# Four cross-attention layers: masked steps taken four at a time, row maxima and denominators spread by way of DRAM

## The chip, the cores and the metric

The kernel runs on one core of a Trainium2 chip. The metric is the device time of one launch in microseconds (us). The engines are PE (TensorE, the matrix products; its weight loads are a row of their own, PEld), DVE (VectorE), ACT (ScalarE), POOL (GpSimd) and SP (SyncE, which here only issues transfers). PE writes to PSUM alone; POOL cannot reach PSUM.

## The reference

`x` (2048 queries of 256 values) passes through four cross-attention layers with a residual each. The keys and values come from one context of 1601 rows of 512 values. Layers 0, 2 and 3 are alike, each with its own weights, 16 heads of 64:

```python
q = hidden_states @ Wq            # 2048 x 1024
k = encoder_hidden_states @ Wk    # 1601 x 1024
v = encoder_hidden_states @ Wv
logits = jnp.einsum('bhqd,bhkd->bhqk', q, k) * scale
col_bias = col_bias.at[:, token_indices_A].set((-SUPPRESS * suppress_A_in)[:, None])
col_bias = col_bias.at[:, token_indices_B].set((-SUPPRESS * suppress_B_in)[:, None])
probs = jax.nn.softmax(logits + col_bias[None, None, :, :], axis=-1)
out = jnp.einsum('bhqk,bhkd->bhqd', probs, v)
out = out.transpose(0, 2, 1, 3).reshape(B, HW, HEADS * HEAD_DIM) @ Wo + bo + residual
```

Four context columns per layer get a bias that depends on the query's mask. Layer 1 has no mask: it takes an RMS norm of `x`, 16 heads of 16 for the queries and 4 heads for keys and values, and the same softmax and residual. All of it is in float32.

## The kernel before

The masked layers (class `Masked`) are cut into blocks of two heads (`n`, 8 of them) and each block into four units of 512 queries. The 12 special context columns of all layers are appended to the context, so a unit has 1613 keys: 13 chunks of 128 (the last has 77). One chunk of one unit is a step, and step numbers run on from unit to unit over the whole kernel. For each step, in time:

- `front` (L400): PE forms the scores of 128 keys by 2 heads by 512 queries in one PSUM tile `s` (two tiles in all). `front_act` (L421, L417 for the first chunk) has ACT copy them to a tile `p` of a ring of 22 in SBUF; `front_dve` (L429) has DVE keep a running maximum `top` over the chunks, per key row.
- after the last chunk, `top_pe` (L438) transposes `top` in two groups of four, `top_dve` (L443) reduces each to the negative maximum of each query, and `spread_pe` (L449) transposes a broadcast of it with eight products into a PSUM tile `mb`, in which every row holds the maxima of all queries.
- 16 steps after the front, `subtract` (L460, L458 for the first chunk): DVE adds `mb` to `p`. `exc` masks the columns that the layer replaces.
- 18 steps after it, `exp_act` (L466): ACT takes the exponential in place; then `exp_pool` (L474, L472): POOL adds the tile to `sums`.
- 20 steps after it, `attend` (L482): PE multiplies by the values into one PSUM tile `po`. After the last chunk `take` (L489) copies it to `o`.

Denominators follow a unit's end: `den_pe` (L300, through `halves`) forms the column sums of `sums` as 16 narrow products, `den_dve` (L503) takes reciprocals, `den_act` (L507) and `scale_pe` (L515) spread them by four transposes, `scale_dve` (L518) multiplies `o`. `out_pe` (L300) and `out_dve` (L527, L532) project and add to the residual `xT`.

Keys and values of the next block are formed during this one: `fill` cuts that into 14 pieces (`keys`, `values`, L300), which read the transposed context `ctxT`, held whole in SBUF. The queries of the next unit are such a piece too, from a copy of the layer's input in DRAM (`snap`, loaded to `xq` at L892).

The order of every engine's instructions is written out by hand: calls in `pin` keep the program's order. The main loop takes two steps at a time (a pair). In a pair stand: the two fronts; their copies and maxima; one piece (`mid`); the two value products; one more piece (`end`); the exponentials and then the subtractions of older steps. `place` puts a piece at a step or in the first later pair that is free; a pair has one `mid` and one `end`.

The grouped layer (class `Grouped`) has the same loop, but finds the maxima in a first pass of transposed scores (L726, L741) and forms the scores again (L775, L780) for the exponential (L788).

PSUM has room for eight banks: two score tiles and `mb` of two banks each, `po` and a tile `pm` of one, which all pieces share.

Of the kernel before, what the change touches and what calls it, by code (L numbers as in the profile page):

```python
# [26 lines left out]
RING = 22  # L27


SUB, EXP, VAL = 16, 18, 20  # L30
DEN, SCALE, OUT, REST = 34, 36, 38, 43
# [7 lines left out]
def tile_cross_attention_stack(ctx: ExitStack, tc: tile.TileContext, t: dict, out: bass.AP):  # L39
# [26 lines left out]
    ps_s = ctx.enter_context(tc.tile_pool(name="ps_s", bufs=2, space=PSUM))  # L66
    ps_b = ctx.enter_context(tc.tile_pool(name="ps_b", bufs=1, space=PSUM))
# [5 lines left out]

    def wide_tile():
        return ps_b.tile([P, 2, QB], FP, name="mb")
# [16 lines left out]
    ctxT = const.tile([P, NCT, TE], FP, name="ctxT")  # L92
# [134 lines left out]
    def load_context(c):  # L227
        n = min(P, T - c * P)
        rows = ring_tile().rearrange("p a b -> p (a b)")[:, :CT]
        nc.sync.dma_start(out=rows[:n, :], in_=cond[0, c * P : c * P + n, :])  # L230
        pt = ps_m.tile([P, NCT, P], FP, name="pm")
        for k in range(NCT):
            nc.tensor.transpose(pt[:, k, :n], rows[:n, ts(k, P)], ident[:n, :n])
        if c % 2:
            nc.vector.tensor_copy(ctxT[:, :, c * P : c * P + n], pt[:, :, :n])
        else:
            nc.scalar.copy(ctxT[:, :, c * P : c * P + n], pt[:, :, :n])

    def load_extra():
# [5 lines left out]
        nc.vector.tensor_copy(ctxT[:, :, T:TE], pt[:, :, :NX])  # L245
# [29 lines left out]
    max_cols = [const.tile([P, QT, P], FP, name=f"max_cols{i}") for i in range(2)]  # L275

    def grouped_constants():
# [10 lines left out]
        for c in max_cols:  # L288
            nc.gpsimd.memset(c, 0.0)
# [3 lines left out]


# [7 lines left out]
    class Masked:  # L302
# [25 lines left out]
        def fill(self, u):  # L328

            found = []  # L330
            for a, n in spans(TE, 256):
                found.append((NCT * n, *self.keys(u, a, n)))
            for c0 in range(0, NT, 2):
                found.append((NCT * P * min(2, NT - c0), *self.values(u, c0, min(2, NT - c0))))
            return found

        def keys(self, u, a, n):
            box = []

            def pe():  # L340
                pk = ps_m.tile([P, QB], FP, name="pm")
                for k in range(NCT):
                    halves(
                        pk[:, :n], u.wk[:, k, :], ctxT[:, k, a : a + n],
# [9 lines left out]
        def values(self, u, c0, n):  # L354
# [3 lines left out]
            def pe():  # L358
                pv = ps_m.tile([P, 4, P], FP, name="pm")
                for c in range(c0, c0 + n):  # L360
                    for k in range(NCT):
                        halves(
                            pv[:m, c - c0, :],
                            ctxT[:, k, c * P : c * P + m], u.wv[:, k, :],
# [70 lines left out]
        def top_pe(self, w, h):  # L435
            w.pt = ps_m.tile([P, QT, P], FP, name="pm")
            for q in range(QT):
                pin(nc.tensor.transpose(w.pt[:, q, :], w.top[:, h, ts(q, P)], ident))  # L438

        def top_dve(self, w, h):  # L440
            if h == 0:
                w.ntop = small.tile([P, 2, QT], FP, name="ntop")
            pin(nc.vector.tensor_reduce(w.ntop[:, h, :], w.pt, AX.X, ALU.max, negate=True))  # L443

        def spread_pe(self, w):
            w.mb = wide_tile()
            for h in range(2):
                for q in range(QT):
                    pin(nc.tensor.transpose(  # L449
                        w.mb[:, h, ts(q, P)],  # L450
                        w.ntop[:, h, q : q + 1].to_broadcast((P, P)), ident,
                    ))
# [15 lines left out]
        def exp_pool(self, w, c):  # L468
            m = P if c < NT - 1 else TAILX
            if c == 1:  # L470
                w.sums = work.tile([P, 2, QB], FP, name="sums", bufs=1)
# [15 lines left out]
        def take(self, w):  # L487
            w.o = work.tile([P, QB], FP, name="o")
            pin(nc.scalar.copy(w.o, w.po))  # L489

# [43 lines left out]
    class Grouped:  # L534
# [3 lines left out]
        def __init__(self, l):  # L538
            self.l = l
            self.xn = {}  # L540
# [46 lines left out]
        def fill(self, u):  # L587
            found = []
            if u.n == 0:
                for a, n in spans(T, 256):  # L590
                    found.append((NCT * n, *self.keys(u, a, n)))
                for c0, n in [(0, 4), (4, 4), (8, 4), (12, 1)]:
                    found.append((NCT * 64 * n, *self.values(u, c0, n)))
            return found

        def keys(self, u, a, n):
            box = []

            def pe():
                pk = ps_m.tile([P, QB], FP, name="pm")  # L600
                for k in range(NCT):
                    pin(nc.tensor.matmul(
                        pk[:64, :n], self.wk[:, k, :], ctxT[:, k, a : a + n],
# [26 lines left out]
        def values(self, u, c0, n):  # L630
# [3 lines left out]
            def pe():  # L634
# [5 lines left out]
                for c in range(c0, c0 + n):  # L640
                    for k in range(NCT):
                        pin(nc.tensor.matmul(
                            pv[:m, c - c0, :], ctxT[:, k, c * P : c * P + m], self.wv[:, k, :],
# [70 lines left out]
        def front(self, w, i):  # L714
            u = w.u
            s = w.tile()
# [32 lines left out]
        def top_cols(self, w):  # L749
            ntop = small.tile([P, 2, QT], FP, name="ntop")  # L750
            pin(nc.vector.tensor_reduce(ntop, w.top, AX.X, ALU.max, negate=True))
            w.cols = max_cols[w.w % 2]
# [16 lines left out]
        def again(self, w, c):  # L769
            u = w.u  # L770
            m = P if c < NT - 1 else TAIL
            s = w.tile()
# [29 lines left out]
        def take(self, w):  # L802
            if w.pair == 0:
                self.o = work.tile([P, QB], FP, name="o")
# [44 lines left out]
    class Unit:  # L849
        def __init__(self, w):  # L850
# [11 lines left out]

        turn = 0

        def tile(self):
            both = self.alone
            if not both:
                return score_tile() if not self.wide else wide_tile()
            Unit.turn += 1
            return wide_tile() if Unit.turn % 3 == 0 else score_tile()  # L870
# [34 lines left out]
    for c in range(NT):  # L905
        load_context(c)
    load_extra()
# [5 lines left out]
    fill = deque(layers[0].fill(made[0]))  # L913
    for _ in range(len(spans(TE, 256))):
        _, pe, then = fill.popleft()
        pe()
        then()


    class Piece:  # L920
        def __init__(self, cost, pe, act=None, dve=None, pool=None):
            self.cost, self.pe, self.act, self.dve, self.pool = cost, pe, act, dve, pool

    mid, end = {}, {}
    snap_after = {}
    early = {}

    tops = {(NT * w + NT - 1) // 2 + 1 for w in range(NU)}
# [225 lines left out]
```

## Time and profile before

| | us |
|---|---|
| runs | 4931.58, 4923.04, 4931.13 (median 4931.13) |
| profiled execution | 4932.33 |
| its span | 4930.6 |
| layer 0, masked (about) | 90 to 1400 |
| layer 1, grouped (about) | 1400 to 2345 |
| layers 2 and 3, masked (about) | 2300 to 4914 |

How to read the lines shown further on: a row of the timeline has its start in us, its length, engine, line of the kernel, operation, tiles written and read, how many such instructions follow each other and, in brackets, how long the engine was idle before and what ended it. A matrix product in float32 stands there as two instructions. The page's 40 slices give the busy tenths of each engine; `PEclk` is the clock that TensorE was granted:

```
PE   6999999999878989888999999999999999999997
DVE  3788888888876666654788888888888888888896
ACT  2666666667645555555666666667676676666675
POOL 0677677667751221120667776767667676767777
PEclk7999999999989999999999999999999999999998
```

### The profile page before, as it was taken

The numbers are of one execution on the slowest core, as the hardware profiler recorded it, in microseconds if no ns is written. First come the engines' busy times: TensorE is split into PE (matmuls) and PEld (weight loads), VectorE is DVE, ScalarE is ACT, GpSimd is POOL, SyncE is SP. The second block draws the span as 40 slices with busy tenths as digits, with TensorE's granted clock in tenths as the row PEclk, the third lists the DMA queues.
The fourth block names the chain that finished last, engine by engine and source line by source line (L and its number), as shares of the span: only waits on it lengthen the run. The fifth ranks groups of instructions, "written<-read, shape, count | busy, mean of one in ns | idle before, by whom it ended". The sixth has DMA issues, their size and how long they took to land.

```text
span 4930.6 us, 72879 instructions
## 1 busy us (share of the span) xinstructions
PE 4570.5 (93%) x29467; PEld 1955.8 (40%) x29467; DVE 3820.4 (77%) x3771; ACT 3191.3 (65%) x3709; POOL 2912.7 (59%) x1481
## 2 busy tenths in 40 slices
PE   6999999999878989888999999999999999999997
PEld 3443444344333333334443444344434443344432
DVE  3788888888876666654788888888888888888896
ACT  2666666667645555555666666667676676666675
POOL 0677677667751221120667776767667676767777
PEclk7999999999989999999999999999999999999998
DMA  2000000000011000000000000000000000000000
GB/s 81 13 18 19 17 20 18 19 17 23 17 26 36 12 18 17 11 21 20 14 20 17 19 20 18 19 17 20 18 23 13 24 18 20 16 20 20 15 9 18
DMA packets 77334, 98.89 MB, mean 20 GB/s; under 512 B 15481, under 2 KB 54905, under 8 KB 76998
## 3 DMA queue, kind: packets, MB, share of 16 engines
q1 hardware_dynamic: 65766, 80.43, 5.4%
q0 software_dynamic: 9120, 11.72, 1.2%
q8 instruction: 232, 3.80, 0.3%
q10 hardware_dynamic: 2112, 2.10, 0.1%
q14 instruction: 104, 0.85, 0.1%
HBM read 80.80 MB, written 13.40 MB: 19 GB/s over the span
## 4 chain that ended last, share of the span: by engine, by line
PE 66%; DVE 18%; ACT 8%; issue 3%; POOL 3%; DMA 0%; POOLq 0%; SPq 0%; DVEq 0%; ACTq 0%
PE pm L300 20%; PE s L400 16%; PE po L482 14%; DVE top L429 7%; DVE p L460 7%; PE po L796 4%; ACT p L788 3%; POOL sums L472 2%; ACT p L421 2%; PE pm L438 2%; PE s L726 1%; PE s L775 1%; ACT p L466 1%; PE mb L449 1%; PE mb L775 1%
## 5 line engine op out<-in xcount | busy, mean ns | idle before, releaser
L474 POOL TENSOR_TENSOR sums<-sums,p 128x1024 f32<-128x1024 f32 (+1 forms) x1056 | 2502.9, 2370 | 510.5 <-ACT p L466 458.1
L429 DVE SCALAR_TENSOR_TENSOR top<-s,exc,top 128x1024 f32<-128x1024 f32 (+1 forms) x1056 | 1351.7, 1280 | 524.7 <-ACT p L421 498.7
L421 ACT COPY p<-s 128x1024 f32<-128x1024 f32 (+1 forms) x1152 | 1129.8, 1014 | 689.3 <-PE s L400 338.6
L460 DVE SCALAR_TENSOR_TENSOR p<-p,exc,mb 128x1024 f32<-128x1024 f32 (+1 forms) x1152 | 1417.8, 1272 | 0.0
L400 PE MATMUL s<-qT,kT 64*128 64x512 f32 (+1 forms) x4992 | 1282.8, 622 | 92.6 <-DVE top L429 87.6
L466 ACT ACTIVATE p<-p 128x1024 f32<-128x1024 f32 (+1 forms) x1248 | 1253.6, 1057 | 21.8 <-DVE p L460 20.7
L482 PE MATMUL po<-p,v 128*64 128x512 f32 (+1 forms) x4992 | 1215.0, 607 | 6.0 <-ACT p L466 5.2
L400 PEld LDWEIGHTS s<-qT,kT 64*128 64x128 f32 (+1 forms) x4992 | 414.7, 183 | 737.2 <-issue 458.9
L472 POOL TENSOR_TENSOR sums<-p 128x1024 f32<-128x1024 f32 x96 | 226.8, 2363 | 748.0 <-PE pm L300 628.0
L482 PEld LDWEIGHTS po<-p,v 128*64 128x64 f32 (+1 forms) x4992 | 328.6, 138 | 503.6 <-issue 425.5
L741 DVE TENSOR_REDUCE gtop<-s 128x2 f32<-128x1024 f32 x261 | 316.7, 1220 | 128.9 <-PE s L726 127.6
L708 POOL DMA_DIRECT2D qT<-gqueries x256 | 124.0, 499 | 458.4 <-PE s L780 298.0
L788 ACT ACTIVATE p<-s 128x1024 f32<-128x1024 f32 (+1 forms) x267 | 270.0, 1023 | 141.2 <-PE s L780 137.4
L300 PE MATMUL pm<-wv,ctxT 128*64 128x128 f32 (+1 forms) x4992 | 348.5, 276 | 10.6 <-DVE o L518 6.6
L300 PEld LDWEIGHTS pm<-wv,ctxT 128*64 128x64 f32 (+1 forms) x4992 | 279.2, 135 | 161.5 <-issue 67.7
L300 PE MATMUL pm<-ctxT,wk 128*64 128x256 f32 (+1 forms) x2688 | 297.4, 363 | 8.8 <-DVE o L518 5.2
L796 PE MATMUL po<-p,v 128*32 128x512 f32 (+1 forms) x1664 | 248.4, 629 | 1.9 <-ACT rx L808 1.8
L300 PEld LDWEIGHTS pm<-ctxT,wk 128*64 128x64 f32 x2688 | 168.0, 136 | 194.6 <-issue 60.2
L741 DVE TENSOR_REDUCE gtop<-mb 128x2 f32<-128x1024 f32 x123 | 150.2, 1221 | 76.0 <-PE mb L726 75.3
L300 PE MATMUL pm<-o,wo 128*64 128x512 f32 x768 | 204.6, 611 | 4.0 <-DVE xT L532 2.5
L788 ACT ACTIVATE p<-mb 128x1024 f32<-128x1024 f32 (+1 forms) x149 | 152.5, 1024 | 79.2 <-PE mb L780 77.2
L532 DVE TENSOR_TENSOR xT<-pm,xT 128x512 f32<-128x512 f32 x168 | 115.1, 685 | 84.3 <-PE pm L300 84.2
(160 smaller groups left out, 3361.1 us busy)
## 6 DMA issues: line engine op xcount, KB each, us to landing
xq<-snap SPq DMA_DIRECT2D x84, 512.0 KB
qT<-gqueries POOLq DMA_DIRECT2D x256, 32.0 KB, 2.0
wk<-in_L_xattn_Wk_dram SPq DMA_DIRECT2D x24, 256.0 KB
wv<-in_L_xattn_Wv_dram SPq DMA_DIRECT2D x24, 256.0 KB
snap<-xT SPq DMA_DIRECT2D x12, 512.0 KB
gqueries<-xq SPq DMA_DIRECT2D x16, 256.0 KB
kT<-gkeys POOLq DMA_DIRECT2D x16, 200.2 KB, 3.9
wq<-in_L_xattn_Wq_dram SPq DMA_DIRECT2D x24, 128.0 KB
```

The source lines that it names most:

```text
L300: pin(nc.tensor.matmul(to[a:e], weights_ap[:, a:e], moving, **kw))
L400: pin(nc.tensor.matmul(s[:m, h, :], u.kT[r, c * P : c * P + m], w.q[r, :], start=True, stop=(c < NT - 1),))
L421: pin(nc.scalar.copy(w.p[c][:m], w.s[c][:m]))
L429: pin(nc.vector.scalar_tensor_tensor(w.top[:m], w.s[c][:m], self.exc[:m, c : c + 1], before[:m], ALU.add, ALU.max,))
L460: pin(nc.vector.scalar_tensor_tensor(p, p, self.exc[:m, c : c + 1], w.mb[:m], ALU.add, ALU.add))
L466: pin(nc.scalar.activation(w.p[c][:m], w.p[c][:m], AF.Exp))
L472: pin(nc.gpsimd.tensor_tensor(w.sums, w.p[0], w.p[1], ALU.add))
L474: pin(nc.gpsimd.tensor_tensor(w.sums[:m], w.sums[:m], w.p[c][:m], ALU.add))
L482: pin(nc.tensor.matmul(w.po[r, :], w.u.v[:m, c, r], w.p[c][:m, h, :], start=(c == 0), stop=(c == NT - 1),))
L741: pin(nc.vector.tensor_reduce(w.top[:, :, q, k : k + 1], w.s[i], AX.X, ALU.max))
L788: pin(nc.scalar.activation(w.p[c][:m], w.s[c][:m], AF.Exp))
L796: pin(nc.tensor.matmul(w.po[ts(j, 32), :], self.v[:m, c, w.u.g, :], w.p[c][:m, h, :], start=(c < 2), stop=(c >= NT - 2),))
```

## The change

Six things change; the lines below are those that the prediction speaks of, and "..." stands for what is left out.

Where the steps are masked alone, the loop takes four at a time (`quad`): three fronts, the first copy and maximum, the fourth front, the other copies and maxima; four value products with up to four pieces between them; then for each of four older steps the subtraction, the exponential and POOL's addition, right behind each other, with the pieces' own ACT and DVE work between. Around the grouped layer the loop stays with pairs (`pair_of`). Subtraction and exponential both stand 16 steps behind the front.

The maxima are transposed in one group of eight into a score tile, reduced once, written to DRAM and read back by all 128 rows into `mb`, which is now a tile of SBUF. PSUM's freed banks make a third score tile.

The denominators are formed by two products of 512 columns with a weight of ones, copied, sent through DRAM to 128 rows for the reciprocal, and through DRAM again to all rows; POOL multiplies `o` by them. The last block of each layer keeps the old way.

The transposed context goes to DRAM in seven slices; each piece of `fill` gets its slice back by a transfer that ACT issues, two slices ahead. RING is 23; `sums` and `o` have two buffers. The start forms the first keys while it loads the context.

```diff
-RING = 22
-SUB, EXP, VAL = 16, 18, 20
+RING = 23
+SUB, VAL = 16, 20
...
-    ps_s = ctx.enter_context(tc.tile_pool(name="ps_s", bufs=2, space=PSUM))
-    ps_b = ctx.enter_context(tc.tile_pool(name="ps_b", bufs=1, space=PSUM))
+    ps_s = ctx.enter_context(tc.tile_pool(name="ps_s", bufs=3, space=PSUM))
...
+class Fill:
...
+        def load(self):
+            self.cs = slice_tile()
+            n = slices[self.i][1]
+            pin(nc.scalar.dma_start(out=self.cs[:, :, :n], in_=ctxD[self.i]))
...
-        def spread_pe(self, w):
-            w.mb = wide_tile()
+        def top_pe(self, w):
+            w.pt = score_tile().rearrange("p h (q r) -> p h q r", r=P)
             for h in range(2):
                 for q in range(QT):
...
+                    pin(nc.tensor.transpose(w.pt[:, h, q, :], w.top[:, h, ts(q, P)], ident))
+        def top_dve(self, w):
+            ntop = small.tile([P, 2, QT], FP, name="ntop")
+            pin(nc.vector.tensor_reduce(ntop, w.pt, AX.X, ALU.max, negate=True))
+            to = tops[w.w % 2]
+                nc.sync.dma_start(out=to.rearrange("h q p -> p h q"), in_=ntop)
+            w.mb = work.tile([P, 2, QB], FP, name="mb", bufs=2)
+            nc.sync.dma_start(
+                out=w.mb,
+                in_=to.rearrange("h q p -> (h q p)").rearrange("(o f) -> o f", o=1)
+                .to_broadcast((P, 2 * QB)),
+            )
...
-            w.o = work.tile([P, QB], FP, name="o")
+            w.o = work.tile([P, QB], FP, name="o", bufs=2)
...
+        def row_pe(self, w):
+            w.pd = ps_m.tile([P, QB], FP, name="pm")
+            for h in range(2):
+                pin(nc.tensor.matmul(
+                    w.pd[64 * h : 64 * h + 64, :], ones[:, 0:64], w.sums[:, h, :],
+                    start=True, stop=True,
+                ))
+        def row_act(self, w):
+            pin(nc.scalar.copy(rows, w.pd))
+            nc.sync.dma_start(
+                out=to[0], in_=rows.rearrange("(h r) q -> h r q", r=64)[:, 0, :]
+            )
+            nc.sync.dma_start(out=w.d8, in_=to[0].rearrange("h (p j) -> p h j", j=QT))
+        def row_dve(self, w):
+            pin(nc.vector.reciprocal(w.d8, w.d8))
+            nc.sync.dma_start(out=to[1].rearrange("h (p j) -> p h j", j=QT), in_=w.d8)
+            for h in range(2):
+                nc.sync.dma_start(
+                    out=w.rx[64 * h : 64 * h + 64, :],
+                    in_=to[1][h : h + 1, :].to_broadcast((64, QB)),
+                )
+        def row_pool(self, w):
+            pin(nc.gpsimd.tensor_tensor(w.o, w.o, w.rx, ALU.mult))
...
+    def quad(q):
...
+        for f in fronts[:3]:
+            f[0].layer.front(*f)
+        for f in fronts[:1]:
+            copies(f)
+        for f in fronts[3:]:
+            f[0].layer.front(*f)
+        for f in fronts[1:2]:
+            copies(f)
+        if soon_top:
+            top.layer.top_pe(top)
...
+        def exponent(i):
+            for f in subs[i : i + 1]:
+                f[0].layer.subtract(*f)
+                f[0].layer.exp_act(*f)
+                f[0].layer.exp_pool(*f)
+        order = [(turns[i], i) for i in sorted(after)]
+        for i in range(5):
+            for turn, at in order:
+                if turn == i:
+                    upto(at)
+                    piece = after[at]
+                    if piece.dve:
+                        piece.dve()
+                    if piece.act:
+                        piece.act()
...
+            if i < 4:
+                exponent(i)
+        if top and not soon_top:
+            top.layer.top_pe(top)
+            top.layer.top_dve(top)
```

## The prediction

> **What bounds the kernel now.** I read the page's busy rows first, then two stages of equal work, then one pair of steps in order of time. Columns of the stage rows: stage, its us, busy us (instructions) of PE, weight load, DVE, ACT, POOL, then TensorE's granted clock, DMA share, GB/s.
>
> ```profile
> PE 4570.5 (93%) x29467; PEld 1955.8 (40%) x29467; DVE 3820.4 (77%) x3771; ACT 3191.3 (65%) x3709; POOL 2912.7 (59%) x1481
> 2505.40:2666.10 160.70, 154.09 (x1018) 65.74 (x1016) 134.63 (x124) 111.48 (x131) 112.72 (x49) 1.00 0.07 19
> 1500.00:2130.00 630.00, 564.05 (x3576) 238.51 (x3572) 408.94 (x463) 360.81 (x402) 129.94 (x230) 0.95 0.08 17
> ```
>
> The second row is one head pair of a masked layer: four units of 13 steps, 160.7 us, 40.2 a unit, 12.36 per four steps. PE is busy for 154.1 of it (38.5 a unit), DVE for 134.6. The third is the grouped layer; its loops stay as they are.
>
> ```profile
> 2514.44 1.99 PE L400 MATMUL s<-qT,kT 64*128 64x512 f32 x8
> 2515.50 2.46 DVE L460 SCALAR_TENSOR_TENSOR p<-p,exc,mb 128x1024 f32<-128x1024 f32 x2
> 2515.67 1.93 ACT L421 COPY p<-s 128x1024 f32<-128x1024 f32 x2 [1.85 <-PE s L400]
> 2516.36 1.95 PE L300 MATMUL pm<-ctxT,wk 128*64 128x256 f32 x16
> 2517.88 2.66 DVE L429 SCALAR_TENSOR_TENSOR top<-s,exc,top 128x1024 f32<-128x1024 f32 x2
> 2518.14 1.89 PE L482 MATMUL po<-p,v 128*64 128x512 f32 x8
> 2518.62 2.00 ACT L466 ACTIVATE p<-p 128x1024 f32<-128x1024 f32 x2
> 2519.95 1.09 PE L449 MATMUL mb<-ident,ntop 128*128 128x128 f32 x8
> 2520.97 1.99 PE L400 MATMUL s<-qT,kT 64*128 64x512 f32 x8
> ```
>
> PE follows itself without a hole from 2514.44 to 2520.97: the pair is paced by PE. DVE subtracts while the scores run; the exponentials at 2518.62 belong to earlier subtractions, so no engine waits in a circle.
>
> **What PE saves.** Per unit: the spread L449 (2519.95 to 2520.97, 1.02); the scale transposes L515 (0.66, and a change of shape, about 0.2 since scores take 1.92 to the next group but 4 x 0.43 of streaming); half the score/value changes (one of 0.2 saved per four steps, 0.65); the second group of top transposes (0.2). The denominators' 32 column products took 1.10 and become two 512-wide ones at 0.86. Together 2.9: 38.5 becomes 35.6 a unit.
>
> **What takes PE's place: a circle through ACT and DVE.** Before, an exponential ran two steps after its subtraction. Now ACT's order in four steps is copy x4, exp x4, DVE's is max x4, subtract x4, and exp 3 stands ahead of the next four's copy 0. The built order also says what waits: a max waits for the copy of its tile, an exp for its subtraction. So: copy 0 (1.01, L421), 0.06 of semaphore, three maxima 1.38 apart (two at 2517.88 take 2.66, 1.28 the last), 1.20 from the fourth to the first subtraction, three subtractions 1.19 apart (two at 2515.50 take 2.46) and the last 1.27, then 0.06 and exp 3 at 1.06. 1.07 + 4.14 + 1.20 + 3.57 + 1.27 + 1.12 = 12.37. That is as long as four steps take today, with PE no longer the reason. Over four units (13 quads): 160.8; plus four output additions between subtractions at 0.7 (L532 0.685), four reciprocals at 0.2, two wide reductions ahead of a max at 1.22 (L741's form; the other two fall while DVE waits for copy 0), one 0.6 for an L489 copy ahead of a late copy; less the maxima that each unit's first chunk does not have (0.25 to 1.38 by position, 3.4 in all): 164.0 against 160.7.
>
> **What mb in SBUF costs.** mb moves from PSUM to SBUF, so all 13 subtractions of a unit read two tensors of SBUF while POOL adds. The trace has that form once, L675 (xT and parts, both SBUF); the lines are DVE, then POOL, at two places.
>
> ```profile
> L675 DVE SCALAR_TENSOR_TENSOR xq<-xT,normw,parts x8: 737/752/2822, 1349.2 to 1505.4; 128x512 f32<-128x512 f32 x8
> 1349.23 1.98 DVE L675 SCALAR_TENSOR_TENSOR xq<-xT,normw,parts 128x512 f32<-128x512 f32 x1
> 1348.32 2.34 POOL L474 TENSOR_TENSOR sums<-sums,p 128x1024 f32<-128x1024 f32 x1 [4.88 <-ACT p L466]
> 1350.74 2.67 POOL L474 TENSOR_TENSOR sums<-sums,p 77x1024 f32<-77x1024 f32 x1
> 1462.69 0.75 DVE L675 SCALAR_TENSOR_TENSOR xq<-xT,normw,parts 128x512 f32<-128x512 f32 x1
> L474 POOL TENSOR_TENSOR sums<-sums,p x1056: 2335/2369/2705, 136.9 to 4910.8; 128x1024 f32<-128x1024 f32 x160, 77x1024 f32<-77x1024 f32 x16
> ```
>
> Alone it takes 0.75. At 1349.23 it meets an addition that ends at 1350.66 and itself ends at 1351.21, 0.55 later, just its stream: it had waited. The next addition, at 1350.74, takes 2.67 for 2.37: POOL waited for DVE, and went on 0.38 after its own last end. The second L675 then waited for that addition (2.82). So they take turns, an operation at a time, the waiting one next. L429 and L460 read one SBUF and one PSUM tensor; 1.28 and 1.27, they never show this. A 1024-wide subtraction so ends 1.08 after the addition that it met, and holds POOL for 0.38 + 0.53 = 0.91.
>
> A quad, from its first subtraction: subtractions at 0, 1.19, 2.38; exp 0 ends 2.39, addition 0 asks at 2.45, just after subtraction 2, and runs 3.4 to 5.8; subtraction 3, at 3.57, meets it and ends at 6.88, not 4.84: +2.04. The other three additions (7.1) fit the 7.5 until the next first subtraction. With an output addition between subtractions 1 and 2, addition 0 is first: subtraction 2 ends at 5.90, addition 1 has waited and takes until 8.1, subtraction 3 ends at 9.18, not 5.56: +3.6. Nine quads and four: 18.4 + 14.4. The new multiplication on POOL (1.26, L809's row) comes behind the three and reaches 0.7 into the next subtractions, once a unit: 2.8. Four units: 164.0 + 32.8 + 2.8 = 199.6, which is 38.9 more. Ends: nothing (POOL always yields), and two additions in every quad, 13 x 4.34 and the output additions hidden: 220.4.
>
> The Trainium skill, "SBUF — State Buffer", section "SBUF: two separate sides", speaks against this edit: a VectorE operation with two SBUF inputs and a GpSimd operation that reads SBUF lock each other out, whoever starts first for its whole instruction. With whole instructions a unit would need 13 x 1.27 + 12 x 2.37 + 1.26 = 46.2 of that lock; the 0.91 of the rows makes it 41.5, already over 40.2.
>
> **Edits costed at nothing.** Each with its cover. (a) Maxima by way of DRAM: reduce, 1024 values of 4 bytes out (L471), 512 KB in (L473), both on SP. Nearest rows: columns of 256 values land after 4.9 to 5.7, a 200 KB stack after 3.9, so about 9.6; cover is three steps, 9 or more at the new pace; uncovered it stops DVE at a unit's first subtraction, and the exps behind it: 0 to 3 a unit, taken as 0. (b) Denominators: five more transfers on SP, ahead of xq's and the weights' loads, which are asked 20 steps early; the waits lie in front of POOL's multiplication, two quads later; behind that stand the next additions, and PE's output product (L327 after) waits for it: 5 of transfers against some 15, and each us over costs a us once a unit, 90. (c) Context slices: 14 loads of 512 KB per head pair from ACT's queue, issue 0.40 each (L249's median), 1.4 a unit, before an exp that waits for its subtraction anyway; else 0.4 per quad. DMA is 0.07 busy. (d) Third score tile, second sums and o, RING 23: they let PE run ahead; PE has 35.6 of some 50. (e) The start and the grouped layer: same instructions, less than 10 either way. (f) TensorE's clock was granted 1.00 in the second row above and 0.95 in the third, where PE idles more; it will idle more now, and needs 35.6 / 50 = 0.71 before it paces.
>
> **The sum.** Stages like the one shown fill 120 to 1320 and 2310 to 4700, 3590 us, 22.3 head pairs. 22.3 x 38.9 = 868. The profiled execution took 4932.3 us (span 4930.6), as good as the median 4931.13 of the runs: 5800.
>
> **Rivals.** (1) The lock does not bite: POOL's additions always fall behind the subtractions. For: it is idle for 48 of 160.7. Against: all four L675 that met an addition, or were met, show a loss. 164.0: +3.3 x 22.3, 5005. (2) It bites twice a quad: if addition 0 is always first; 2.38 and 2.45 are too close to tell. 220.4: +59.7 x 22.3, 6260. (3) The mb transfers come late, by 3 to 5 a unit on top: 6070 to 6250. (4) Faster, the other side: PE still paces, with fewer changes of shape. For: 93% busy now. It takes (35.6 x 4 + today's 6.6 idle) = 149.0, 11.7 x 22.3 less, 4670. It decides only where the circle is under 11.5 a quad and the lock costs nothing; against it stands the order exp 3, copy 0, max 0. (5) That steps are not taken by four: the built order has four scores, then values, so no.
>
> **Chances.** Mine 0.60, (1) 0.13, (2) 0.15, (3) 0.07, (4) 0.05. 5800 is my own sum; its own range, with addition 0 late in some quads or early in others, is 5400 to 6100. Down to 5200 and up to 6260 it takes in most of (2) and (3) and leaves out (1), (4), about 0.2. Faster by over 0.2% (what this kernel's runs can tell from no change) is (4), 0.05; within 0.2%, 0.02 out of (1); slower 0.93.
>
> **What would show it.** In the profile after: the subtraction's mean well over 1.27 (about 1.9: 13 x 1.27 and 32.8 / 4 of waiting per unit, over 13) and POOL's addition over 2.37; PE busy about 70% in masked stages, its idle time ended by DVE's maxima; a head pair near 200. L675-like waits absent and a head pair near 164 is (1); DVE's first subtraction waiting for mb's landing is (3); PE over 90% busy is (4). I am wrong altogether if a max starts before the copy of its tile ends.

## The result and the profile after

The changed kernel takes 6425.9 us (median of 4 runs, 6413.0 to 6438.0), the kernel before beside it 4930.1 (4 runs): 1496 us more, a ratio of 1.304 with a 95% interval of 1.301 to 1.307. The direction was forecast, the size was not: 5800 was 626 short, and the time lies above the range.

The page's busy row and its clock slices for the changed kernel come first, then two head pairs of a masked layer and the grouped layer as stages (columns as in the prediction).

```profile
PE 4800.0 (75%) x26011; PEld 1929.3 (30%) x26011; DVE 4334.0 (67%) x3591; ACT 3237.3 (50%) x3709; POOL 3441.7 (54%) x1564
PEclk7888889888888999998888888888988888888887
```

```profile
3893.80:4115.10 221.30, 163.93 (x859) 63.76 (x858) 157.24 (x117) 113.57 (x131) 139.26 (x53) 0.88 0.25 58
4115.10:4337.00 221.90, 164.10 (x858) 64.27 (x856) 154.16 (x117) 113.58 (x130) 136.97 (x53) 0.88 0.24 58
1850.00:2760.00 910.00, 781.81 (x5028) 333.54 (x5032) 605.01 (x657) 503.90 (x571) 226.45 (x325) 0.94 0.12 29
```

A head pair takes 221.6, not 160.7 and not the 199.6 of the forecast. No engine is full: TensorE works 74% of the stage, VectorE 70%. TensorE is busy for longer than before (164.0 for 154.1) although it has less to do, at a granted clock of 0.88 for 1.00. The stretch between the last masked copy of layer 0 and the first of layer 2, in which the grouped layer lies, is unchanged: 912 before, 907 after. The whole loss lies in the masked layers: 55.4 us a unit for 40.0, by the first and last copy of layers 2 and 3.

The groups of instructions of the changed kernel (busy, mean of one, idle time before and what ended it):

```profile
L485 DVE SCALAR_TENSOR_TENSOR p<-p,exc,mb 128x1024 f32<-128x1024 f32 (+1 forms) x1152 | 1906.7, 1705 | 0.0
L499 POOL TENSOR_TENSOR sums<-sums,p 128x1024 f32<-128x1024 f32 (+1 forms) x1056 | 2899.9, 2746 | 1476.4 <-ACT p L491 1410.5
L483 DVE TENSOR_TENSOR p<-p,mb 128x1024 f32<-128x1024 f32 x96 | 136.6, 1423 | 279.7 <-DMA mb<-tops 279.7
L446 ACT COPY p<-s 128x1024 f32<-128x1024 f32 (+1 forms) x1152 | 1110.6, 1012 | 764.1 <-PE po L507 681.1
```

The subtraction went from 1272 to 1705 ns, the addition from 2370 to 2746: they take turns, as forecast. A unit's first subtraction (L483) now waits 279.7 us in all for the maxima to come back from DRAM, which was forecast at nothing. And the copies wait 681 us for a value product (`po`), which no step of the prediction had.

One group of four in order of time, with its neighbours, in the changed kernel:

```profile
4006.76 0.36 SPq L471 DMA_DIRECT2D tops<-ntop  x1
...
4008.94 6.92 DVE L485 SCALAR_TENSOR_TENSOR p<-p,exc,mb 128x1024 f32<-128x1024 f32 x4
...
4011.41 11.51 POOL L499 TENSOR_TENSOR sums<-sums,p 128x1024 f32<-128x1024 f32 x4 [4.97 <-ACT p L491]
4015.89 1.06 ACT L491 ACTIVATE p<-p 128x1024 f32<-128x1024 f32 x1 [2.23 <-DVE p L485]
4016.85 2.82 ACT L446 COPY p<-s 128x1024 f32<-128x1024 f32 x3
4017.88 4.06 DVE L454 SCALAR_TENSOR_TENSOR top<-s,exc,top 128x1024 f32<-128x1024 f32 x3 [2.02 <-ACT p L446]
4019.22 2.08 PE L425 MATMUL s<-qT,kT 64*128 64x512 f32 x4 [5.64 <-DVE top L454]
4019.41 0.33 SPq L473 DMA_DIRECT2D mb<-tops  x1
...
4021.23 3.68 PE L507 MATMUL po<-p,v 128*64 128x512 f32 x8
4023.30 1.01 ACT L446 COPY p<-s 128x1024 f32<-128x1024 f32 x1 [3.63 <-PE po L507]
4024.35 1.28 DVE L454 SCALAR_TENSOR_TENSOR top<-s,exc,top 128x1024 f32<-128x1024 f32 x1 [2.40 <-ACT p L446]
...
4037.04 1.13 PE L425 MATMUL s<-qT,kT 64*128 64x512 f32 x4 [2.18 <-DVE top L454]
```

Four subtractions take 6.92: the forecast of 6.88 for this kind of group is met. Exp 3 ends at 4016.95 and copy 0 follows at 4016.85 (the rows overlap a little): the circle is there. But the fourth copy starts 6.45 after the first, and the fourth maximum 7.5 after it instead of 5.2: TensorE has idled 5.64, takes 2.08 for a score that takes 1.13 at 4037.04, and the copy is let go only by the value product behind the score. The maxima's way out, issued at 4006.76, lets the way in be issued at 4019.41, 12.7 later.

### The profile page after: what moved, and what is told of

Same layout as the page of the kernel before. It is cut to its first block, busy times and chain, and to the rows that moved or that the text cites. A ratio compares the mean times of both kernels' runs of the same rounds, so it can differ in the third digit from the quotient of the medians.

```text
span 6422.5 us, 67813 instructions
## 1 busy us (share of the span) xinstructions
PE 4800.0 (75%) x26011; PEld 1929.3 (30%) x26011; DVE 4334.0 (67%) x3591; ACT 3237.3 (50%) x3709; POOL 3441.7 (54%) x1564
## 4 chain that ended last, share of the span: by engine, by line
PE 33%; DVE 26%; DMA 15%; ACT 14%; issue 8%; POOL 4%; SPq 0%; ACTq 0%; POOLq 0%; DVEq 0%
DVE p L485 13%; DMA tops<-ntop 9%; PE po L507 9%; DVE top L454 8%; PE s L425 7%; ACT p L446 7%; PE pm L327 6%; DMA mb<-tops 4%; PE po L858 3%; POOL sums L499 3%; ACT p L850 3%; ACT p L491 2%; DMA dens<-d 2%; PE s L837 1%; PE s L784 1%
## 5 line engine op out<-in xcount | busy, mean ns | idle before, releaser
L499 POOL TENSOR_TENSOR sums<-sums,p 128x1024 f32<-128x1024 f32 (+1 forms) x1056 | 2899.9, 2746 | 1476.4 <-ACT p L491 1410.5
L485 DVE SCALAR_TENSOR_TENSOR p<-p,exc,mb 128x1024 f32<-128x1024 f32 (+1 forms) x1152 | 1906.7, 1705 | 0.0
L507 PE MATMUL po<-p,v 128*64 128x512 f32 (+1 forms) x4992 | 1486.4, 713 | 22.6 <-ACT o L514 16.9
L799 DVE TENSOR_REDUCE gtop<-s 128x2 f32<-128x1024 f32 x384 | 464.6, 1221 | 170.9 <-PE s L784 168.5
L850 ACT ACTIVATE p<-s 128x1024 f32<-128x1024 f32 (+1 forms) x416 | 412.9, 1022 | 204.5 <-PE s L842 202.5
L327 PE MATMUL pm<-cs,wk 128*64 128x256 f32 (+1 forms) x2688 | 323.6, 386 | 137.2 <-ACT rx L527 80.4
L327 PE MATMUL pm<-wv,cs 128*64 128x128 f32 (+1 forms) x4992 | 354.6, 280 | 9.6 <-ACT qT L414 3.5
L327 PEld LDWEIGHTS pm<-wv,cs 128*64 128x64 f32 (+1 forms) x4992 | 301.8, 139 | 141.2 <-issue 114.5
L483 DVE TENSOR_TENSOR p<-p,mb 128x1024 f32<-128x1024 f32 x96 | 136.6, 1423 | 279.7 <-DMA mb<-tops 279.7
L327 PEld LDWEIGHTS pm<-cs,wk 128*64 128x64 f32 x2688 | 189.7, 146 | 324.7 <-ACT rx L527 113.8
L784 PE MATMUL s<-kT,qT 64*128 64x512 f32 (+1 forms) x1024 | 197.3, 409 | 52.7 <-ACT p L850 48.2
```

The source lines that it names most:

```text
L327: pin(nc.tensor.matmul(to[a:e], weights_ap[:, a:e], moving, **kw))
L485: pin(nc.vector.scalar_tensor_tensor(p, p, self.exc[:m, c : c + 1], w.mb[:m], ALU.add, ALU.add))
L499: pin(nc.gpsimd.tensor_tensor(w.sums[:m], w.sums[:m], w.p[c][:m], ALU.add))
L507: pin(nc.tensor.matmul(w.po[r, :], w.u.v[:m, c, r], w.p[c][:m, h, :], start=(c == 0), stop=(c == NT - 1),))
L784: pin(nc.tensor.matmul(s[:, h, at : at + n], w.q[r, ts(q, P)], u.kT[r, a : a + n], start=True, stop=True,))
L799: pin(nc.vector.tensor_reduce(w.top[:, :, q, k : k + 1], w.s[i], AX.X, ALU.max))
```

## The experiments

Each kernel was run once beside the kernel before (4920 to 4935), and the last one four times. Differences under some 30 us are not read, as the changed kernel's own runs spread over 25.

### One cost at a time

**Additions left out** (e1). The sums are set to one, so the outputs are not normalised; GpSimd adds nothing.

```diff
-                pin(nc.gpsimd.tensor_tensor(w.sums, w.p[0], w.p[1], ALU.add))
-            elif c:
-                pin(nc.gpsimd.tensor_tensor(w.sums[:m], w.sums[:m], w.p[c][:m], ALU.add))
+                pin(nc.gpsimd.memset(w.sums, 1.0))
```

> The changed kernel with POOL's additions left out: sums is set to one once a unit, so denominators are wrong; all else is as changed. Theory A (three costs add up: subtractions that wait for POOL's turn in SBUF, a fourth copy that waits for a value product, maxima that land late): subtractions fall from 1.70 to 1.27 on average, a head pair of blocks from 221.6 by about 13 x 2 = 26 to 196, the whole to about 5850. Rival B (PE at a lower clock and its order set the pace, the waiting on DVE is cover): subtractions fall too, but a head pair stays over 212, the whole over 6200.

Measured: 5897.1, 529 less, with a subtraction of 1291 ns:

```profile
L485 DVE SCALAR_TENSOR_TENSOR p<-p,exc,mb 128x1024 f32<-128x1024 f32 (+1 forms) x1152 | 1429.6, 1291 | 0.0
```

All subtractions together are busy 496 us less than in the changed kernel (1429.6 + 117.3 for 1906.7 + 136.6), so taking turns accounts for nearly all of these 529 of 1496.

**Maxima written in runs of 32 bytes** (e3), which permutes them among the queries: the same 4 KB in 128 pieces instead of 1024.

```diff
-                nc.sync.dma_start(out=to.rearrange("h q p -> p h q"), in_=ntop)
+                nc.sync.dma_start(
+                    out=to.rearrange("h q p -> (h q p)").rearrange("(p f) -> p f", f=2 * QT),
+                    in_=ntop.rearrange("p h q -> p (h q)"))
```

> The 1024 maxima of a unit are written to DRAM as 128 runs of 32 bytes and not as 1024 of 4; they then belong to other queries, which the softmax allows, and nothing else changes. Theory A: the transfer lands in about 3 and not 11.4, the first subtraction's 280 of waiting in all is gone, the whole falls by 150 to 280, to 6150 to 6280. Rival: the wait comes from the order of SP's queue, where the reading stands behind the denominators' transfers: the 11.4 and the time stay.

Measured: 6151.6, 274 less. The second transfer is issued 2.7 us (median) after the first instead of 11.4, and the first subtraction no longer waits; its row in this run:

```profile
L486 DVE TENSOR_TENSOR p<-p,mb 128x1024 f32<-128x1024 f32 x96 | 116.9, 1217 | 0.0
```

**The second SBUF operand alone, in the kernel before** (e4, and e7 as its control). The maxima are spread into PSUM as before, then ScalarE copies them to SBUF (room is made by keeping the grouped layer's columns in another tile). In e4 the subtraction reads the copy; e7 lacks the last line below, and it goes on reading PSUM.

```diff
+        def spread_copy(self, w):
+            mb = work.tile([P, 2, QB], FP, name="mbs", bufs=1)
+            pin(nc.scalar.copy(mb, w.mb))
+            w.mb = mb
```

> The kernel before with one part of the change: mb is copied by ACT to SBUF after the spread (1.0 a unit) and read from there; two constant tiles lie elsewhere to make room. Theory A: subtractions take 1.5 or more on average and POOL's additions over 2.5; a pair of steps needs 2 x 2.37 + 2 x 0.91 = 6.56 of turns where it has 6.18, so a head pair of blocks takes 171 or more, the whole 5150 to 5800. Rival (taking turns costs nothing that others don't hide): within 40 of before.

> The kernel before with the maxima copied from PSUM to SBUF as in the run that took 5951, but with the subtraction still reading them from PSUM. Theory A: the 1029 of that run came from the subtraction's second SBUF operand alone (its mean went from 1272 to 2200 ns, x1152 = 1069): here 4920 to 5010 with a mean near 1.27. Rival B: the copy on ScalarE or the moved column tile costs a good part of it: over 5150.

Measured: 5950.8, which is above the range of e4's Theory A, and 4931.2. Their subtractions, e4 first:

```profile
L462 DVE SCALAR_TENSOR_TENSOR p<-p,exc,mbs 128x1024 f32<-128x1024 f32 (+1 forms) x1152 | 2489.0, 2200 | 0.0
```

```profile
L461 DVE SCALAR_TENSOR_TENSOR p<-p,exc,mb 128x1024 f32<-128x1024 f32 (+1 forms) x1152 | 1417.9, 1272 | 0.0
```

The operand alone costs 1020, and 1152 x 0.928 us more of subtraction is 1069. This is the cleanest pair of the study: a copy that is made in both, and read in one. The 529 of e1 is another quantity (additions left out, in another order), so the two do not say that the operand costs twice as much by pairs: in e12 below, by pairs too, the subtraction takes 1379 ns.

### The order by four

**The fourth copy ahead of the first value product** in the order of emission (e2), and **two value products ahead of the fourth score** on TensorE (e5).

```diff
+        for f in fronts[3:]:
+            copies(f)
         values(1)
         take(1)
         if soon_top:
             top.layer.top_dve(top)
-        for f in fronts[3:]:
-            copies(f)
```

```diff
+        ahead = 1 if end == 1 else 2
+        for i in range(1, ahead + 1):
+            values(i)
         for f in fronts[3:]:
             f[0].layer.front(*f)
...
-        values(1)
```

> The fourth copy and maximum of four steps are written ahead of the first value product, nothing else. Theory A: the copy then waits for its own scores and not for a value product; the fourth maximum starts 5.2 to 5.7 after the first copy instead of 6.6 to 7.5, 1.5 x 13 = 20 a head pair, the whole at about 5980. Rival B: what is gained is lost again where subtractions meet more of POOL's additions, less than 100 in all.

> The changed kernel with the first two value products of a group of four issued on TensorE ahead of the fourth score, in the time in which TensorE otherwise waits for the first maximum. Theory A: the fourth maximum starts 6.6 to 7.5 us after the first copy, not 5.2, because TensorE idles 2 to 4 us, runs on at half clock (0.50), and copy 3 is released by a value product emitted ahead of it (copy 3 put ahead of the first value in the order of the other engines was no gain: TensorE's own order had stayed). With the gap filled the fourth maximum starts 5.2 to 6 after copy 0, 1 to 2 us less in each of 312 groups: 5800 to 6120. Rival B: a group is set by the subtractions held up by GpSimd's additions and by exp 3, whatever TensorE does before: within 60 of 6426.

Measured: 6461.5 and 6329.2. In e2 nothing had moved: TensorE's own order stayed, and copy 3 still starts when the value product ends, as this row of it shows:

```profile
4039.34 1.01 ACT L446 COPY p<-s 128x1024 f32<-128x1024 f32 x1 [3.63 <-PE po L507]
```

In e5 the gap was filled in the typical group: its last maximum starts 5.6 after copy 0 (median; 6.9 in the changed kernel). Yet only 97 came of it, outside both ranges. In the mean over 199 groups of layers 2 and 3 the first subtraction comes 7.44 after copy 0 for 7.75, because the slowest tenth of the groups have their last maximum at 8.5 or later, for 7.5. The subtractions take as long as before (8.06 for 8.09 a group, mean). So Theory A had the wait right and its worth wrong; why some groups became later was not settled.

**Maxima in PSUM again, by four** (e6), which leaves two score tiles and one tile for the grouped layer's second scores, and **every step by pairs** (e12), with all else of the change kept.

```diff
-    ps_s = ctx.enter_context(tc.tile_pool(name="ps_s", bufs=3, space=PSUM))
+    ps_s = ctx.enter_context(tc.tile_pool(name="ps_s", bufs=2, space=PSUM))
+    ps_b = ctx.enter_context(tc.tile_pool(name="ps_b", bufs=1, space=PSUM))
...
             if c == 0:
+                self.spread_pe(w)
```

```diff
     def by_pairs(q):
-        return any(grouped_step(s) or grouped_step(s - SUB) for s in range(4 * q, 4 * q + 4))
+        return True
```

> The changed kernel, still by four, with the negated maxima spread by transpositions into PSUM as before (no transfer through DRAM, subtraction with one SBUF operand), and two score tiles instead of three. Theory A: taking turns with the additions (about 529) and the transfer of the maxima (about 274) fall away, and what remains, some 690 of 1496, is the order by four itself with TensorE's gaps: 5550 to 5900, with about 2 us a unit for the transpositions that wait for the last subtraction of the unit before. Subtraction mean back near 1.27. Rival B: the order by four costs next to nothing once subtraction and transfer are right: 4930 to 5300.

> The changed kernel with every step run in the order by pairs that it keeps for the grouped layer: maxima and denominators through DRAM, context in slices and three score tiles stay. Theory A: by pairs, subtractions and maxima of different steps fill each other's waits, but the subtraction's second SBUF operand still costs what it cost in the kernel before with the maxima in SBUF (50.6 us a unit, 5951), and late maxima about 2 to 3 a unit more: 5950 to 6250, below 6426. Rival B: the order by four is what made up for the slower parts, and by pairs they cost more: over 6426.

Both theories of e6 missed: 6537.5. Its subtraction is back at 1269 ns and no subtraction waits for DRAM, but the last maximum of a group starts 8.2 after copy 0 (median), and a unit takes 54.9 for 55.4; the grouped layer lost 174 besides. In the masked layers next to nothing is won: the four subtractions take 6.0 for 8.1 a group (mean), but the first of them comes 9.3 after copy 0 for 7.75, and the units' first subtractions wait 166 us in all for the transpositions. That the missing third tile is behind the later maximum is an argument; it was not changed alone. e12 took 6575.2, in the range of Rival B but not for its reason. The rows show why:

```profile
4031.20 1.11 SPq L541 DMA_DIRECT2D rx<-dens  x2
4035.01 1.26 POOL L547 TENSOR_TENSOR o<-o,rx 128x512 f32<-128x512 f32 x1 [5.28 <-DMA rx<-dens]
4036.33 1.98 PE L327 MATMUL pm<-o,wo 128*64 128x512 f32 x4 [10.93 <-POOL o L547]
...
4038.96 1.22 DVE L483 TENSOR_TENSOR p<-p,mb 128x1024 f32<-128x1024 f32 x1
...
L327 PE MATMUL pm<-o,wo 128*64 128x512 f32 x768 | 296.5, 861 | 919.1 <-POOL o L547 883.2 <-DVE xT L590 28.4 <-DVE o L576 7.4
```

The denominators' last transfer is issued behind the maxima's, and TensorE idles 10.93 for the scaled output. The last row is the group over the whole run: 883.2 us of such waits, where the changed kernel has 24. The subtraction takes 1379 ns here. In this order, too, each exp directly follows its subtraction. It is not the order of the kernel before, so e12 does not price the step from pairs to four.

**No additions, and maxima turned into 8 rows** (e11): one transposition of the 128 x 8 negated maxima, a copy, 8 rows of 512 bytes. What is left is the order by four with its three score tiles, the denominators by way of DRAM and the context slices.

```diff
+            pin(nc.tensor.transpose(pr[: 2 * QT, :], w.ntop.rearrange("p h q -> p (h q)"), ident))
+            rows = small.tile([2 * QT, P], FP, name="nrows")
+            pin(nc.vector.tensor_copy(rows, pr[: 2 * QT, :]))
+            nc.sync.dma_start(out=to.rearrange("h q p -> (h q) p"), in_=rows)
```

> The changed kernel with GpSimd's additions left out (the sums are set to one) and the maxima turned and written as 8 rows of 512 bytes: neither the taking of turns nor most of the late maxima is left, and the three score tiles and the order by four stay. Theory A: a group of four is one circle (copy 0, the last maximum's end 7.4 us later, the subtractions 4.9, the last exp 1.1 to 1.4, then copy 0 again), 13.8 to 14.6 us, 45 to 47.5 a unit against 40.2 before: 5400 to 5680, that is, the order by four alone costs 470 to 750 of 1496. Rival B: the circle closes only where the others are late, and by four alone is as fast as by two: under 5150.

Measured: 5616.1, as Theory A had it: 685 above the kernel before, with neither turns nor late maxima. The two of them together in the changed kernel (e8) gave less:

> As the run with two values first, and the maxima turned by one transposition and written as 8 rows of 512 bytes instead of 1024 pieces of 4 bytes. Theory A: both gains add up, 274 from the transfer and 300 to 600 from the filled gap: 5550 to 5870. Rival B: only the transfer's part shows: 6100 to 6200.

Measured: 6285.5, 44 below e5 and outside both ranges. With the fourth score early, the maxima in rows bring little: the subtractions of a group take 7.47 for 8.06 (mean), but copy 0 follows exp 3 after 0.64 for 0.23.

**Two exponentials deferred**, in the changed kernel (e16), with the rows (e17), and without additions (e19). Exps 2 and 3 of a group run in the next group, after its second copy.

```diff
         for f in fronts[1:2]:
             copies(f)
+        flush()
...
-                f[0].layer.exp_act(*f)
-                f[0].layer.exp_pool(*f)
+                if i < 2:
+                    f[0].layer.exp_act(*f)
+                    f[0].layer.exp_pool(*f)
+                else:
+                    held_exps.append(f)
```

> The changed kernel with the exponentials (and additions) of the third and fourth subtraction of a group run in the next group, after its second copy, as the kernel before ran each exponential one pair after its subtraction. Theory A: the order by four costs because copy 0 stands behind exp 3 and exp 3 behind subtraction 3, so that ScalarE and VectorE take turns; without it copies 0 and 1 lie beside the last two subtractions, and of the 17.2 us of a group the exp (1.2) and the copy with its delay (1.0 to 1.3) leave the circle, less what copies 2 and 3 lose behind two exps: 1 to 2.5 in 312 groups, 5650 to 6110. Rival B: the fourth score or GpSimd sets the group whatever ScalarE's order is: within 60 of 6426.

> The run without additions and with maxima in rows (5616), and the same two exponentials deferred. Theory A: nothing of the 47.4 us a unit is left but VectorE's own eight instructions in four steps and TensorE's products: 4850 to 5300, near the kernel before. Rival B: the order by four costs its 685 through the fourth score and TensorE's clock, not through the exponentials: over 5550.

> The changed kernel with the two exponentials deferred and the maxima turned and written as 8 rows, additions and all outputs kept. Theory A: both gains add up: 5400 to 5850. Rival B: what the exponentials give comes back as longer turns between subtractions and additions: 6100 to 6300.

Measured: 6210.9, 5417.6 and 5988.7: 215, 198 and 437 less than what they started from. All three lie between the ranges of the two theories: the exponentials are a part of it, not all. The circle is opened, as two groups of e19 show:

```profile
4028.76 1.93 ACT L446 COPY p<-s 128x1024 f32<-128x1024 f32 x2 [0.61 <-PE s L425]
4029.80 2.67 DVE L454 SCALAR_TENSOR_TENSOR top<-s,exc,top 128x1024 f32<-128x1024 f32 x2 [0.62 <-ACT p L446]
4030.57 2.02 ACT L496 ACTIVATE p<-p 128x1024 f32<-128x1024 f32 x2
...
4036.14 4.86 DVE L490 SCALAR_TENSOR_TENSOR p<-p,exc,mb 128x1024 f32<-128x1024 f32 x4
...
4040.51 1.93 ACT L446 COPY p<-s 128x1024 f32<-128x1024 f32 x2 [0.55 <-PE s L425]
```

From copy 0 to copy 0 it is 11.75, below the 12.36 of four steps before, and copy 0 starts while subtractions still run. Over layers 2 and 3 the mean group goes from 17.2 to 16.5 in e16 and from 14.7 (e11) to 14.1 in e19. Sorted by what stands among its instructions on VectorE, a group without an output addition or a reduction of maxima takes 11.75 in e19 (median of 79) and 12.0 in e17, one with an output addition 15.9 and 18.1. In e16 the first kind shows no gain: 17.1, as in the changed kernel. What e17 still pays is in two rows of it, VectorE and GpSimd in the same stretch:

```profile
4001.27 11.75 DVE L490 SCALAR_TENSOR_TENSOR p<-p,exc,mb 128x1024 f32<-128x1024 f32 x4
3999.68 12.26 POOL L504 TENSOR_TENSOR sums<-sums,p 128x1024 f32<-128x1024 f32 x4
```

Four subtractions beside four additions: 11.75 instead of 4.86. Each waits for an addition.

**Output additions later** (e20, on top of e17): in groups with one or two side pieces, behind the second subtraction. The line moves all of a piece's work on VectorE and ScalarE, so the copies that ScalarE makes of new keys and values move too.

```diff
-        turns = {1: 0, 2: 1, 3: 2, 4: 4} if len(pieces) > 2 else {1: 0, 2: 0, 3: 1, 4: 3}
+        turns = {1: 0, 2: 1, 3: 2, 4: 4} if len(pieces) > 2 else {1: 2, 2: 2, 3: 2, 4: 4}
```

> The run with exponentials deferred and maxima in rows (5989), and in groups with one or two side pieces the output addition on VectorE moved from ahead of the first (or second) subtraction to behind the second. In that run a group without output addition or maximum reduction takes 11.8 us (median), one with an output addition 17.8. Theory A: the addition waits on VectorE for a product that stands behind two value products on TensorE, and the four subtractions wait behind it: 1 to 3 us less in some 140 of 312 groups, 5560 to 5850. Rival B: these groups are long because their subtractions meet the additions on GpSimd, and the place of the output addition moves the time only: 5900 to 6050.

Measured: 6191.2, 202 more, outside both. Sorted as above, groups with an output addition went from 18.1 to 17.6 and those without an addition or a reduction from 12.0 to 16.2. The run does not test the additions alone: TensorE now waits 125 us for the copies of new keys and 60 for those of new values, where e17 has none and 2.

### A part that pays

**The denominators through DRAM, alone, in the kernel before** (e13). `row_pe`, `row_act`, `row_dve` and `row_pool` of the change are taken over, the second `o` tile with them, and the output products come five pairs after the rows. The grouped layer's columns lie in another tile, as in e4.

```diff
-        place(mid, t0 + DEN, Piece(
-            512, lambda: ly.den_pe(un), act=lambda: ly.den_act(un), dve=lambda: ly.den_dve(un)))
-        place(mid, t0 + SCALE, Piece(256, lambda: ly.scale_pe(un), dve=lambda: ly.scale_dve(un)))
+            at = place(mid, t0 + DEN, Piece(
+                512, lambda: ly.row_pe(un), act=lambda: ly.row_act(un)))
+            early.setdefault(at + 2, []).append(lambda: ly.row_dve(un))
+            early.setdefault(at + 4, []).append(lambda: ly.row_pool(un))
+            out_at = 2 * at + 10
```

> The kernel before with one part of the change alone: the denominators by way of DRAM (four products with ones on TensorE, rows to DRAM, reciprocal, back spread over 64 partitions, multiplication on GpSimd) in place of 16 products, 4 transpositions and a multiplication on VectorE. Theory A: TensorE paces that kernel in its masked stages and loses about 1 us a unit: 4830 to 4910. Rival B: GpSimd's multiplication and the later output projections cost as much as is saved: 4920 to 5000.

Measured: 4879.4 (4 runs, 4874.8 to 4888.2) for 4934.6, a ratio of 0.989 (0.987 to 0.991). This version is 1.1% faster than the kernel before, with the interval clear of one. Its page:

```profile
PE 4532.3 (93%) x26779; PEld 1902.4 (39%) x26779; DVE 3782.5 (77%) x3687; ACT 3192.4 (65%) x3709; POOL 3011.0 (62%) x1564
```

TensorE is busy 38 us less than before (4570.5) and paces as it did; a unit takes 39.6 for 40.0.

## Why the prediction was right and wrong

The mean parts of a group of four, in us, from the starts and ends of its instructions in layers 2 and 3 (199 groups each). The forecast's row is its circle alone; with output additions, reciprocals and reductions it had 164.0 / 13 = 12.6 without turns, and 199.6 / 13 = 15.4 with them.

| | copy 0 to first subtraction | subtractions | to end of exp 3 | to copy 0 | sum |
|---|---|---|---|---|---|
| forecast, no turns | 6.4 | 4.8 | 1.1 | 0.0 | 12.4 |
| changed kernel | 7.75 | 8.09 | 1.23 | 0.14 | 17.2 |
| e1, no additions | 7.44 | 6.53 | 1.36 | 0.29 | 15.6 |
| e3, maxima in runs | 7.65 | 7.20 | 1.27 | 0.24 | 16.4 |
| e11, neither | 7.24 | 5.61 | 1.35 | 0.54 | 14.7 |

**The kind of bound was right.** TensorE left the path, at 74% of the stage for the 70% forecast, and the circle copy 0, maxima, subtractions, exp 3, copy 0 took its place; deferring two exps opened it (e19's rows) and gave back 198 to 215.

**The length of the circle is the step that failed most.** It was put at 164.0 a head pair, 3.3 above the 160.7 of before, 74 us in all. With turns and late maxima out of the way it is 4 x 47.4 = 189.7 (e11), and 685 is left. The fourth maximum was put at 5.2 from the copy and the spacing of the maxima alone. TensorE was left out of it: the fourth score waits for the first maximum, runs at a lower clock when the gap before it was long, and in the changed kernel its copy is let go by a value product. The first column is 0.8 longer than forecast in e11 and 1.3 in the changed kernel. The subtractions, 5.6 for 4.8 there, hold output additions, which were charged 0.7 each as work and wait for TensorE besides. Of the 685, 198 went with the exps; the other 486 are not placed. In e19 groups without output work are then as short as before (11.75 for 12.36), those with it are not (15.9), and e20 did not settle why. The order by four was not tried in the kernel before by itself, so the 486 may hold other parts of the change.

**The turns were the right mechanism, sized too high.** 35.6 a head pair over 22.3 head pairs is 794; e1 gives 529. The mean of a subtraction was forecast at about 1.9 over all 13 of a unit and is 1.68. That the real group is longer, so that more of the additions fall beside the maxima, would explain the difference. In the shorter groups of e16 and e17 the subtraction takes 1.879 and 1.875, for 1.705 in the changed kernel (L485), which fits; but the order differs there too, and it was not tried by itself. Rival (2), every group held twice at 6260, is nearest in number, but that is luck: the rows at 4008.94 show a single hold, and the median group takes 6.98. Rival (1), no turns, is out by the subtraction's 1705 ns in the changed kernel and 1291 without additions. The rule of the Trainium skill, "SBUF — State Buffer", section "SBUF: two separate sides", was the right warning, and the pair e4 and e7 is what it looks like here: 2200 ns a subtraction for 1272, and 1020 us, for one operand's place.

**Edit (a), the maxima through DRAM, costed at nothing, is the second step that failed.** 9.6 was estimated for both transfers, from columns of 256 values. The 1024 pieces of 4 bytes alone take 11.4 before the next can be issued, and the first subtraction follows 6.8 after that (medians). It waits 279.7 in the profile, and 274 (e3) or 281 (e11 against e1) came back: 2.9 a unit. This was rival (3), which I had set against my own case though nothing kept both from being true. Added, they would have given 6070 and more.

**Edit (f), the clock, was costed at nothing because TensorE had time to spare.** On the path it has none: the fourth score. Filling its gap alone brought 97 (e5), but the granted clock of the whole run fell from 0.88 to 0.86 there, so what the clock costs was not measured.

**Edit (e) held, (b), (c) and (d) stay open.** The grouped layer did not move. The denominators' way through DRAM pays by itself in the kernel before (e13), but GpSimd waits 159 us for it in the changed kernel; what that costs there was not tried alone, nor were the context slices (c) or the third score tile (d). Rival (4), TensorE paces and 4670, is out.

## What to carry to other kernels

When steps are regrouped, look for the offset that kept two engines from waiting on each other: here an exp two steps behind its subtraction. Without turns and late maxima 685 of the 1496 were left, and deferring two of every four exps again returned 198. Where an operand moves from PSUM to SBUF on VectorE, count GpSimd's SBUF time on the same stretch, and test it with a copy that is read and one that is not. A time between pieces of work should be taken as a mean over all groups as well as a median: in e5 the median promised over 1 us a group and the mean gave 0.3. A rival that adds to the forecast belongs in its sum, not beside it.

## What the runs showed of the hardware

- Of 4 KB, 1024 pieces of 4 bytes hold up the next transfer for 11.4 us (median of 96); 128 pieces of 32 bytes, 2.7 (e3); 8 rows of 512 bytes, 2.8 (e17).
- After a gap of 5.64 a score took 2.08, after one of 2.18 it took 1.13 (rows at 4019.22 and 4037.04). Between 2800 and 4650 of the changed kernel, the 24 scores behind gaps of 5 or more all took 2.07 or 2.08, the 23 behind gaps of 0.5 to 2 at most 1.13, and those between were mixed. The Trainium skill, "TensorE: Matmul & The Clock Gate", section "What's actually happening", puts the half-rate clock after an idle window of about 3.4 us; the gaps of 5 and more agree with it. A shorter gap can do it too: in the kernel before, the score at 2496.26 took 2.08 behind a gap of 2.21, at a granted clock of 0.50 from 2496.4 to 2499.6.
- Beside a stream of additions, four subtractions with both operands in SBUF took 2.9 us each (e17): as many additions as subtractions passed, and each subtraction waited for one. With one operand in PSUM, and the same additions in the kernel, a subtraction took 1.27 (e7, mean).
